# Softplus as one function of ScalarE in a four-layer kernel with a Mamba scan

## The chip, the core and the metric

The kernel runs on one core of a Trainium2 chip. The metric is the device time of one execution in microseconds (us), of which the median over several runs is taken. The core's engines work side by side, each through its own queue of instructions and in the order of that queue: PE multiplies matrices, DVE is the vector engine, ACT (ScalarE) evaluates functions, POOL is GpSimd, and SP only issues transfers. They wait for each other through semaphores.

## The reference

Eight images of 384 channels and 32 x 32 pixels pass through four layers. Layer 0 is a Mamba block that goes over the 1024 pixels forwards and backwards; layer 1 is a convolution block with linear attention and an MLP; layers 2 and 3 are 13 x 13 depthwise convolutions with a pointwise layer between them. The change lies in layer 0:

```python
dt, Bm, Cm = jnp.split(x_dbl, [dt_rank, dt_rank + D_STATE], axis=-1)
delta = jax.nn.softplus(jnp.einsum('blr,dr->bld', dt, dt_proj_w) + dt_proj_b)
A = -jnp.exp(A_log)
deltaA = jnp.exp(delta[..., None] * A)
deltaBu = (delta * u)[..., None] * Bm[:, :, None, :]
h = dA * h + dBu          # for each pixel, over 16 states of each channel
```

## The kernel before

All data is fp32. Channels lie on the 128 partitions in NC = 3 chunks (index c), and the 1024 pixels of an image in two halves of 512 (index h); index d is the direction, 0 forwards and 1 backwards.

**Stages.** `_layers01` computes layers 0 and 1 image by image. Three generators do the work of one image b. `front(b)` (line 572) normalizes, projects, convolves and ends with softplus; it writes u (u_d), z, B and C (bc_d), softplus (dl_d, called delta), delta times u (v_d) and a skip term (ud_d) to scratch in DRAM. `scan(b)` (line 695) reads them back, each channel replicated to four partitions for four of the 16 states at a time, and runs the recurrence. `layer1(b)` (line 877) does the output projection and layer 1. At the bottom of `_layers01`, front(0) comes first; then there is one round per image b, in which scan(b) gives the beat and pieces of front(b + 1) and layer1(b - 1) are recorded between its steps, in proportion to costs written by hand (90 and 325). Round 0 has no layer1, round 7 no front; layer1(7) follows the rounds, and then the two convolutions with the pointwise layer (lines 247 to 372).

**Order.** The order in which the lines are recorded is not yet the order in the queues: the framework's scheduler moves instructions at build time, so that for example the end of front(0) and the start of scan(0) are interleaved on every engine.[...] Which of ACT's instructions needs a load of another function table is also settled at build time, and such a load stands in ACT's queue as an instruction of its own.

**The scan.** For each of 12 units (d, h, c) and each of NR = 4 groups of states r, two pairs i of channel groups are treated. ACT computes da = exp(delta times A) (two instructions of 512 columns, line 776), DVE du = v times B (line 781, 1024 columns, into PSUM) and then two scans with `tensor_tensor_scan` (line 793), POOL multiplies the result hs by C (line 802), and PE sums over the states into acc (`sums`, line 736). There are 768 such pairs in all. A small copy (line 798) carries the state from the first half of the pixels to the second.

**Softplus** stands at the end of `front`. For each half h, line 652 projects onto dt, B and C, ACT copies that to xd (line 656), and then for each chunk c and direction d PE expands dt into a PSUM tile (line 667). ACT takes four passes over it: Abs with the bias into t (line 671), Relu with the bias into dl (line 672), exp(-t) (line 676) and ln(1 + t) (line 678), so that Relu plus Ln is softplus. The closure `deltas` is deferred by one `tick`: DVE adds the two (line 683), multiplies by u (line 684, result into t), POOL issues both transfers to DRAM (lines 685 and 686), DVE adds the u of both directions (line 687), and ACT scales that by D and sends it away (lines 689 and 690). Eight fronts with two halves, three chunks and two directions make 96 such tiles.

**Buffers.** `t2` is a ring of eleven SBUF tiles of 128 x 512 that `front` and `layer1` share (the MLP's hm also lives in it): the eleventh tile after takes the buffer again, and whichever instruction first writes it waits for the last reader, often a transfer. `psum` is a ring of two PSUM tiles named "mm", used by the dt matmuls, the projections, the small convolutions and the MLP's first product mf. The MLP of layer 1 alternates PE (mf, line 502), ACT's Gelu (hm, line 1062) and PE (mo, line 1064).

Of the kernel before, what the change touches and what calls it, by code (L numbers as in the profile page):

```python
# [9 lines left out]
AF = mybir.ActivationFunctionType  # L10
# [364 lines left out]
def _layers01(tc, nc, B, xv, x2_d, dram, ident, mean_w, eps5, eps6, one, half, minus1, vec, bns, bnt,  # L375
# [12 lines left out]
    with ExitStack() as ctx:  # L388
# [73 lines left out]
        def t2(name):  # L462
            return sp.tile([P, HALF], FP, tag="t2", name=name, bufs=N_T2)
# [4 lines left out]
        def a6(name):  # L468
            return sp.tile([P, NC, HALF], FP, tag="a6", name=name, bufs=N_A6)
# [80 lines left out]
        def rsqrt_mean(srcs, eps, name):  # L550

            stat = psum(f"{name}_s")
            for k, src in enumerate(srcs):
                for j in range(4):
                    nc.tensor.matmul(
                        stat[32 * j : 32 * j + 32, 0:P], mean_w[:, 0:32], src[:, j * P : (j + 1) * P],
                        start=(k == 0), stop=(k == NC - 1), skip_group_check=True,
                    )
            r = t2(f"{name}_r")[:, 0:P]
            nc.scalar.activation(r, stat[:, 0:P], AF.Ln, bias=eps)  # L560
            nc.scalar.activation(r, r, AF.Exp, scale=-0.5)
            ps = psum(f"{name}_b")
            for j in range(4):
                nc.tensor.matmul(
                    ps[:, j * P : (j + 1) * P], spread[:, j, :], r, start=True, stop=True,
                    skip_group_check=True,
                )
            return ps
# [3 lines left out]
        def front(b):  # L572

            xn = []
            for h in range(2):
                cols = bass.ts(h, HALF)
                xh = a6(f"xi_{b}_{h}")
                nc.sync.dma_start(xh, xv[b][:, :, cols])
                sqs = [t2(f"sq_{b}_{c}_{h}") for c in range(NC)]
                for c in range(NC):  # L580
                    nc.scalar.activation(sqs[c], xh[:, c, :], AF.Square)
                rstd = rsqrt_mean(sqs, eps6, f"ms_{b}_{h}")
                t, mid = image6(f"xn_{b}_{h}")
                for c in range(NC):
                    nc.vector.scalar_tensor_tensor(
                        mid[c], rows(xh[:, c, :]), vec("norm_w", c), rows(rstd), ALU.mult, ALU.mult
                    )
                put_image(xn_d, b % 2, h, t, nc.gpsimd)
                xn.append(mid)
                yield 3  # L590
            uo = u_d[b % 2].rearrange("(c p) i -> p c i", p=P)
            for e in range(2):
                w = wtile(inproj_t[:, e * C : (e + 1) * C], f"win_{b}_{e}")
                for h in range(2):
                    for m in range(NC):
                        ps = psum(f"in_{b}_{e}_{m}_{h}")
                        dense(ps, w, m, xn[h])
                        t = t2(f"uz_{b}_{e}_{h}_{m}")
                        if e == 0:
                            nc.scalar.copy(t, ps)  # L600
                            nc.scalar.dma_start(uo[:, m, 3 + h * HALF : 3 + (h + 1) * HALF], t)
                        else:
                            nc.scalar.activation(t, ps, AF.Silu)
                            nc.scalar.dma_start(zv[b][:, m, bass.ts(h, HALF)], t)
                        yield 3


            t3 = tapw(taps3, f"t3_{b}")
            for h in range(2):
                for c in range(NC):  # L610
                    xr = t2(f"xr_{b}_{h}_{c}")
                    nc.sync.dma_start(xr, xv[b][:, c, bass.ts(h, HALF)])
                    ps = conv3(xn_d, b % 2, h, c, t3, f"lc_{b}_{h}_{c}")
                    lc = t2(f"lg_{b}_{c}_{h}")
                    nc.scalar.activation(lc, ps, AF.Sigmoid, bias=vec("dw_b0", c))

                    def local(h=h, c=c, lc=lc, xr=xr):
                        nc.vector.tensor_mul(rows(lc), rows(lc), xn[h][c])
                        nc.vector.scalar_tensor_tensor(xr, lc, rs, xr, ALU.mult, ALU.add)
                        nc.gpsimd.dma_start(x1v[b][:, c, bass.ts(h, HALF)], xr)  # L620

                    defer(1, local)
                    yield 3


            for h in range(2):
                cols = bass.ts(h, HALF)
                ucs = [a6(f"uc_{b}_{h}_{d}") for d in range(2)]
                for c in range(NC):
                    uts = []  # L630
                    for j in range(4):
                        ut = sp.tile([P, 18 * (W + 2)], FP, tag="im", name=f"ut_{b}_{h}_{c}_{j}", bufs=N_IM)
                        src = bass.AP(
                            u_d.tensor, u_d[b % 2, 32 * (4 * c + j), h * HALF].offset,
                            [[UL, 32], [1, 4], [1, HALF + 3]],
                        )
                        nc.sync.dma_start(ut[:, 0 : HALF + 3], src)
                        uts.append(ut)
                    for d in range(2):
                        ps = psum(f"c1_{b}_{h}_{c}_{d}")  # L640
                        col32(
                            ps, lambda j, i: t1[:, d * NG + 4 * c + j, :],
                            lambda j, i: uts[j][:, 3 * d : 3 * d + HALF], 1,
                        )
                        nc.scalar.activation(ucs[d][:, c, :], ps, AF.Silu, bias=vec("conv1d_b", c))
                    yield 2

                xd = t2(f"xd_{b}_{h}")
                ps = psum(f"xd_{b}_{h}")
                for k in range(NC):  # L650
                    for d in range(2):
                        nc.tensor.matmul(
                            ps[64 * d : 64 * d + 64, :], wx[:, k, :], ucs[d][:, k, :],
                            start=(k == 0), stop=(k == NC - 1), skip_group_check=True,
                        )
                nc.scalar.copy(xd, ps)
                for d in range(2):
                    lo = 64 * d + DTR
                    nc.scalar.dma_start(bc_d[b, d][:, cols], xd[lo : lo + 2 * NST, :])
                yield 3  # L660

                for c in range(NC):
                    dls, ts = [], []
                    for d in range(2):
                        ps = psum(f"dt_{b}_{h}_{d}_{c}")
                        at = slice(64 * d, 64 * d + DTR)
                        nc.tensor.matmul(
                            ps, wdt[at, c * P : (c + 1) * P], xd[at, :], start=True, stop=True
                        )
                        t, dl = t2(f"sp_{b}_{h}_{d}_{c}"), t2(f"dl_{b}_{h}_{d}_{c}")  # L670
                        nc.scalar.activation(t, ps, AF.Abs, bias=vec("dt_b", c))
                        nc.scalar.activation(dl, ps, AF.Relu, bias=vec("dt_b", c))  # L672
                        ts.append(t)
                        dls.append(dl)
                    for t in ts:
                        nc.scalar.activation(t, t, AF.Exp, scale=-1.0)
                    for t in ts:
                        nc.scalar.activation(t, t, AF.Ln, bias=one)

                    def deltas(h=h, c=c, dls=dls, ts=ts, ucs=ucs):  # L680
                        for d in range(2):
                            dl, t = dls[d], ts[d]
                            nc.vector.tensor_add(dl, dl, t)
                            nc.vector.tensor_mul(t, dl, ucs[d][:, c, :])
                            nc.gpsimd.dma_start(dlv[b, d][:, c, bass.ts(h, HALF)], dl)
                            nc.gpsimd.dma_start(vv[b, d][:, c, bass.ts(h, HALF)], t)
                        nc.vector.tensor_add(ucs[0][:, c, :], ucs[0][:, c, :], ucs[1][:, c, :])
                        ud = t2(f"ud_{b}_{h}_{c}")
                        nc.scalar.activation(ud, ucs[0][:, c, :], AF.Copy, scale=vec("D", c))
                        nc.scalar.dma_start(udv[b][:, c, bass.ts(h, HALF)], ud)  # L690

                    defer(1, deltas)
                    yield 3

# [519 lines left out]
```

## Time and profile before

The median is 5797.18 us (5793.76 to 5818.33 over three runs); the profiled execution took 5805.1 us from first to last instruction, at a mean granted PE clock of 0.896.

| stretch (us from the start) | stage | PE busy | DVE busy | ACT busy |
|---|---|---|---|---|
| 150 to 212 | end of front(0) before the scan | 34.4 | 13.2 | 32.2 |
| 212 to 300 | front(0) and scan(0) interleaved | 53.5 | 46.0 | 62.5 |
| 300 to 550 | round 0 | 167.9 | 227.9 | 145.2 |
| 550 to 750 | round 0, softplus of front(1) | 108.7 | 179.4 | 119.3 |
| 4640 to 4785 | layer1(7) | 96.4 | 19.2 | 15.3 |
| 5075 to 5220 | first convolution | 145.0 | 27.1 | 8.6 |

Busy is the time in us in which an engine executed something in the stretch. In the slices of the profile each digit stands for one fortieth of the span, 145 us, in tenths. A group line gives line of code, engine, operation, output and inputs by name, shapes, count, then busy time and mean duration in ns, then the idle time of the engine directly before and what ended it. In the waits view a line reads: who waited (engine, output, line), for whom, us in total, times, longest.

### The profile page before, as it was taken

To read this page: it belongs to the slowest core of one execution; us is meant where nothing else is said; L and a number is where in the kernel's file an instruction comes from. 1 tells how busy PE (TensorE), PEld (TensorE's weight loads), DVE (VectorE), ACT (ScalarE), POOL (GpSimd) and SP (SyncE) were. 2 spreads that over 40 slices of the span, in tenths; PEclk is the share of its full clock that TensorE was granted. 3 is DMA by queue.
4 is the path that set the end of the run, shared out by engine and by line. 5 is a ranking of instruction groups with operands and counts; after the bars stand their busy time and mean duration, and the time that the engine had idled before them with its cause. 6 is when DMAs were issued, how large, how long until landed. Compare 5 with 4: busy or idle time off the path is not lost. (4 is left out here: it accounts for less than half of the span.)

```text
span 5805.1 us, 57844 instructions
## 1 busy us (share of the span) xinstructions
PE 4813.5 (83%) x19550; PEld 2091.8 (36%) x19550; DVE 3677.1 (63%) x3775; ACT 3064.5 (53%) x4116; POOL 2892.9 (50%) x1603
## 2 busy tenths in 40 slices
PE   4576579977988799879888997899779869899999
PEld 1121124322332243223322332233223324498498
DVE  0399997968687768776878786878678811011211
ACT  1656546874667557846784687468635613000211
POOL 3277676557554656565656564656466700110133
PEclk7687689988999899989999998899889989999999
DMA  9555476677567756764666467646643541366677
GB/s 299 185 176 178 145 247 194 230 188 216 187 197 202 216 173 193 168 204 134 191 205 189 141 175 186 190 140 176 179 145 120 135 96 45 95 165 158 196 166 150
DMA packets 528255, 1012.16 MB, mean 174 GB/s; under 512 B 60616, under 2 KB 196248, under 8 KB 527960
## 3 DMA queue, kind: packets, MB, share of 16 engines
q1 hardware_dynamic: 387952, 665.99, 38.5%
q0 software_dynamic: 71136, 248.53, 16.6%
q10 hardware_dynamic: 68872, 93.95, 5.1%
q8 instruction: 155, 2.54, 0.2%
q14 instruction: 140, 1.15, 0.1%
HBM read 763.86 MB, written 288.36 MB: 181 GB/s over the span
## 5 line engine op out<-in xcount | busy, mean ns | idle before, releaser
L802 POOL TENSOR_TENSOR hs<-hs,bct 128x1024 f32<-128x1024 f32 x768 | 2378.7, 3098 | 1180.4 <-DVE hs L793 665.8
L776 ACT ACTIVATE da<-dlt,neg_a 128x512 f32<-128x512 f32 x1536 | 1031.7, 714 | 848.8 <-DVE hs L793 756.8
L793 DVE TENSOR_TENSOR_SCAN hs<-da,carry,du 128x512 f32<-128x512 f32 x768 | 947.1, 1268 | 445.8 <-PE acc L736 211.0
L781 DVE TENSOR_TENSOR du<-vr,bct 128x1024 f32<-128x1024 f32 x768 | 1048.3, 1365 | 51.7 <-issue 21.7
L793 DVE TENSOR_TENSOR_SCAN hs<-da,du 128x512 f32<-128x512 f32 x768 | 901.2, 1208 | 153.9 <-ACT da L776 74.0
L736 PE MATMUL acc<-hs,selt 128*32 128x512 f32 x3072 | 736.5, 674 | 293.0 <-POOL hs L802 241.7
L1064 PE MATMUL mo<-hm,w 128*128 128x512 f32 x1152 | 562.5, 628 | 84.4 <-ACT hm L1062 60.8
L502 PE MATMUL mf<-ln,w 128*128 128x512 f32 x1152 | 545.7, 614 | 42.8 <-ACT dl L672 40.4
L736 PEld LDWEIGHTS acc<-hs,selt 128*32 128x32 f32 x3072 | 122.3, 115 | 722.2 <-POOL hs L802 391.6
L1064 PEld LDWEIGHTS mo<-hm,w 128*128 128x128 f32 x1152 | 214.9, 197 | 427.8 <-issue 255.1
L776 ACT ACT_TABLE_LOAD x265 | 340.0, 1283 | 39.2 <-DVE hs L793 26.7
L502 PEld LDWEIGHTS mf<-ln,w 128*128 128x128 f32 x1152 | 215.2, 194 | 358.9 <-issue 285.1
L316 PE MATMUL cv_b<-xt_b,toep 128*64 128x256 f32 x2688 | 304.5, 388 | 14.1 <-DVE xt_b L298 14.1
L316 PE MATMUL cv_a<-xt_a,toep 128*64 128x256 f32 x2688 | 304.6, 388 | 9.2 <-DVE xt_a L298 9.2
L502 PE MATMUL in<-xn,win 128*128 128x512 f32 x576 | 289.1, 633 | 26.0 <-ACT phi_k L874 24.2
L511 PE MATMUL dw<-dw_i,t3b 96*32 96x512 f32 x1152 | 238.0, 707 | 86.4 <-DMA dw_i<-h_d 86.3
L316 PEld LDWEIGHTS cv_b<-xt_b,toep 128*64 128x64 f32 x2688 | 282.5, 199 | 36.6 <-issue 16.2
L316 PEld LDWEIGHTS cv_a<-xt_a,toep 128*64 128x64 f32 x2688 | 282.4, 199 | 31.1 <-issue 10.4
L511 PE MATMUL lc<-lc_i,t 96*32 96x512 f32 x1152 | 218.1, 679 | 57.2 <-issue 28.8
L511 PE MATMUL c<-ut,t 128*32 128x512 f32 x768 | 195.2, 676 | 45.6 <-DMA ut<-u_d 32.1
L502 PE MATMUL op<-g,wo 128*128 128x512 f32 x288 | 143.1, 647 | 86.7 <-DMA g<-g_d 58.7
L1062 ACT ACTIVATE hm<-mf,biasf 128x512 f32<-128x512 f32 x192 | 130.7, 687 | 145.2 <-PE mf L502 143.5
(189 smaller groups left out, 5618.3 us busy)
## 6 DMA issues: line engine op xcount, KB each, us to landing
dlt<-dl_d SPq DMA_DIRECT2D x384, 256.0 KB, 4.5
vr<-v_d SPq DMA_DIRECT2D x384, 256.0 KB, 4.7
bct<-bc_d SPq DMA_DIRECT2D x256, 256.0 KB, 4.1
ut<-u_d SPq DMA_DIRECT2D x192, 257.5 KB, 5.0
lc_i<-xn_d SPq DMA_DIRECT2D x192, 228.8 KB, 4.9
dw_i<-h_d SPq DMA_DIRECT2D x192, 228.8 KB, 4.1
tp_d<-g_d POOLq DMA_DIRECT2D x64, 672.0 KB, 7.2
w<-w_d SPq DMA_DIRECT2D x64, 576.0 KB, 5.8
```

The source lines that it names most:

```text
L316: nc.tensor.matmul(ps[2 * H * e : 2 * H * (e + 1), 0:BW], tp[:, 2 * (g % (GB // 2)) + e, :, :, t].rearrange("p c j -> p (c j)"), rhs, star ...
L502: nc.tensor.matmul(ps, w[:, k, m * P : (m + 1) * P], rhs[k] if isinstance(rhs, list) else rhs[:, k, :], start=(k == 0), stop=(k == NC - 1),)
L511: nc.tensor.matmul(ps[32 * j : 32 * j + 32, :], lhs(j, i), rhs(j, i), start=(i == 0), stop=(i == taps - 1), skip_group_check=True,)
L736: nc.tensor.matmul(acc[32 * j : 32 * j + 32, :], selt, hs[j // 2][:, bass.ts(j % 2, HALF)], start=(r == 0), stop=(r == NR - 1), skip_group ...
L776: nc.scalar.activation(da[:, bass.ts(j, HALF)], dlt[:, bass.ts(j, HALF)], AF.Exp, scale=neg_a[:, g, r : r + 1],)
L781: nc.vector.tensor_mul(pairs(du), pairs(vt), bct[r][:, 0:1, :].to_broadcast([P, 2, HALF]),)
L793: nc.vector.tensor_tensor_scan(t[:, s][:, way], da[:, s][:, way], du[:, s][:, way], k_c if second else 0.0, ALU.mult, ALU.add,)
L802: nc.gpsimd.tensor_mul(pairs(t), pairs(t), bct[r][:, 1:2, :].to_broadcast([P, 2, HALF]))
L1062: nc.scalar.activation(hm, ps, AF.Gelu, bias=biasf[:, NC * i + f, :])
L1064: nc.tensor.matmul(acc[m], wb[:, f, m * P : (m + 1) * P], hm, start=(i == 0 and f == 0), stop=(i == FF // C - 1 and f == NC - 1),)
```

## The change

ScalarE has Softplus as a function of its own. One activation with the bias now writes dl from PSUM; Abs, Relu, Exp and Ln and DVE's addition are gone. Since t is no longer there when DVE multiplies by u, the closure draws a fresh tile v from the same ring. In the changed program Softplus stands in line 670, the multiplication in line 676, and later lines have numbers smaller by eight. Its purpose is to take passes off ACT and an addition off DVE.

```diff
                 for c in range(NC):
-                    dls, ts = [], []
+                    dls = []
                     for d in range(2):
...
-                        t, dl = t2(f"sp_{b}_{h}_{d}_{c}"), t2(f"dl_{b}_{h}_{d}_{c}")
-                        nc.scalar.activation(t, ps, AF.Abs, bias=vec("dt_b", c))
-                        nc.scalar.activation(dl, ps, AF.Relu, bias=vec("dt_b", c))
-                        ts.append(t)
+                        dl = t2(f"dl_{b}_{h}_{d}_{c}")
+                        nc.scalar.activation(dl, ps, AF.Softplus, bias=vec("dt_b", c))
                         dls.append(dl)
-                    for t in ts:
-                        nc.scalar.activation(t, t, AF.Exp, scale=-1.0)
-                    for t in ts:
-                        nc.scalar.activation(t, t, AF.Ln, bias=one)
-
-                    def deltas(h=h, c=c, dls=dls, ts=ts, ucs=ucs):
+
+                    def deltas(h=h, c=c, dls=dls, ucs=ucs):
                         for d in range(2):
-                            dl, t = dls[d], ts[d]
-                            nc.vector.tensor_add(dl, dl, t)
+                            dl, t = dls[d], t2(f"v_{b}_{h}_{d}_{c}")
                             nc.vector.tensor_mul(t, dl, ucs[d][:, c, :])
```

## The prediction, made before the changed kernel had run

> **What bounds the kernel now.** I first read the page: busy times and slices.
>
> ```profile
> PE 4813.5 (83%) x19550; PEld 2091.8 (36%) x19550; DVE 3677.1 (63%) x3775; ACT 3064.5 (53%) x4116; POOL 2892.9 (50%) x1603
> DVE  0399997968687768776878786878678811011211
> ACT  1656546874667557846784687468635613000211
> ```
>
> Over the span ACT (53%) looks harmless, but the slices show rounds of about four slices in the scan stage (about 212 to 4650 us), and once per round ACT rises to 7 or 8 tenths while DVE falls to 6 or 7. The chain of waits does not help: it reaches back only to 5017 us, through the two convolutions. So I went to the groups by line, for what the change touches:
>
> ```profile
> L678 ACT ACT_TABLE_LOAD x60 | 77.0, 1283 | 1.1
> L671 ACT ACTIVATE sp<-dt,pk 128x512 f32<-128x512 f32 x96 | 65.5, 682 | 106.9 <-PE dt L667 78.1 <-DMA dl_d<-dl 18.3 <-DMA ud_d<-ud 10.4
> L672 ACT ACTIVATE dl<-dt,pk 128x512 f32<-128x512 f32 x96 | 65.4, 681 | 0.1
> L678 ACT ACTIVATE sp<-sp,one 128x512 f32<-128x512 f32 x96 | 65.4, 716 | 0.7
> L676 ACT ACTIVATE sp<-sp 128x512 f32<-128x512 f32 x96 | 57.1, 628 | 0.4
> L676 ACT ACT_TABLE_LOAD x35 | 44.9, 1283 | 0.6
> L683 DVE TENSOR_TENSOR dl<-dl,sp 128x512 f32<-128x512 f32 x96 | 97.0, 1035 | 106.5 <-ACT sp L678 106.5
> ```
>
> Busy and mean duration stand after the first bar, idle time before the group after the second. These rows are all that softplus costs. The windows view then placed them: besides front(0), each of seven fronts has its twelve tiles within a stretch of 160 to 200 us. For the six rounds with both background jobs (1150:1310, 1760:1930, 2310:2480, 2880:3040, 3440:3600, 4020:4180), one row and the sum:
>
> ```profile
> core 0: us, PE busy (x) PEld busy (x) DVE busy (x) ACT busy (x) POOL busy (x), PEclk, DMA share, GB/s
> 2880.00:3040.00 160.00, 137.66 (x391) 44.77 (x390) 125.58 (x113) 139.72 (x174) 95.72 (x59) 0.94 0.64 198
> sum 980.00, PE 780.92 PEld 252.48 DVE 690.38 ACT 779.98 POOL 524.21; mean PE 130.15 PEld 42.08 DVE 115.06 ACT 130.00 POOL 87.37
> ```
>
> ACT is busy 780 of 980 us, as much as PE. Who waits there? From the whole kernel's waits view:
>
> ```profile
> DVE hs L793 <- ACT da L776: 254.0, 82, 16.4
> DVE dl L683 <- ACT sp L678: 106.5, 30, 24.1
> PE mo L1064 <- ACT hm L1062: 60.8, 40, 5.3
> ```
>
> In the six stretches alone, DVE's waits for ACT add up to 231.5 us (45.0, 51.3, 34.9, 27.9, 37.3, 35.1) and PE's to 104.0 us (24.5, 41.7, 8.8, 6.3, 12.4, 10.3). So in the softplus stretches ACT's queue is what the scan on DVE, and partly PE, stands behind; elsewhere it is not.
>
> **What the Trainium skill says.** "ScalarE: Activation LUTs", section "What ACT_TABLE_LOAD costs", prices a load at 1283 ns plus a DRAIN of about 1380 ns, and every function alike, about 93 ns more with a pointer bias. The trace agrees on 1283 ns and on durations (628 ns with immediates, 681 to 716 with a pointer bias), but not on the DRAIN: between the load at 189.24 us and the Exp at 190.54 there is only the load. The same page, section "Table sets: the hidden batching unit", says that Exp and Ln share one set and need one load. The trace differs: 35 loads stand before the Exp of softplus and 60 before the Ln. "Perfetto Trace Analysis", section "Tensor Engine Instruction (MATMUL, LD_WEIGHTS)", says that ACT and DVE are strict FIFO; the trace agrees where scans stop behind a softplus addition (below). No page prices Softplus.
>
> **The change part by part.** *ACT.* Removed: 65.5 + 65.4 + 57.1 + 65.4 = 253.4 us of activations, and 95 loads, 121.9 us. Added: 96 Softplus. The trace has none; from below the fastest op on this PSUM shape is the copy at L600, 577 ns, from above Ln, 716 ns. I take L671's 682 ns, same operands: 65.5 us. The loads I counted in the two built instruction orders: 61 before Softplus (78.3 us), and elsewhere 34 more before the scan's Exp, 3 more before Silu, 6 fewer before Gelu, 2 fewer each at L561 and L1015: 27 more, 34.6 us. In all 776 loads become 769. Net: -253.4 - 121.9 + 65.5 + 78.3 + 34.6 = -196.9 us, or 24.6 us for each of eight fronts.
>
> *DVE.* 96 additions go, 97.0 us: 8.4 in front(0), 16.7 in 550:750, 10.1 to 14.5 in each later stretch.
>
> *Buffers and waits.* Each channel chunk still draws five tiles from the ring of eleven t2, so its length costs nothing; but v's tile is now drawn when DVE multiplies, not when ACT begins. The waits for old transfers at L671 (18.3 + 10.4 us) can thus move to DVE, where the scans queue behind them, and behind those POOL's multiplications and PE's sums. Between zero and one transfer each (4.8 us to landing for v_d): I take zero, since the tile is asked for later than before, and most old ones land within 5 us. The two PSUM tiles "mm" come free after one operation and perhaps a load (0.68 to 1.97 us) instead of two (1.26 us spaced): no change taken. PE, POOL and the transfers keep their work, and their order shifts a little: at the round ends the scan stands up to one unit further ahead of the MLP.
>
> *Where it shows.* (a) front(0), where nothing hides it:
>
> ```profile
> 193.75 1.31 DVE L683 TENSOR_TENSOR dl<-dl,sp 128x512 f32<-128x512 f32 x2 [24.09 <-ACT sp L678]
> 205.70 1.23 DVE L781 TENSOR_TENSOR du<-vr,bct 128x1024 f32<-128x1024 f32 x1 [1.42 <-DMA vr<-v_d]
> 214.88 0.72 ACT L776 ACTIVATE da<-dlt,neg_a 128x512 f32<-128x512 f32 x1
> 215.64 1.22 DVE L793 TENSOR_TENSOR_SCAN hs<-da,du 128x512 f32<-128x512 f32 x1 [3.34 <-ACT da L776]
> ```
>
> ACT's first-half softplus runs from 186.80 to 209.77, and the first scan waits for an Exp behind it. With Softplus the first result is there at about 188.8 instead of 193.7, du about 5.6 us earlier (near 200), and ACT is free by then: first scan near 205, 10 us won. In the second half DVE has no scan from 246.2 to 266.4, its queue held by additions that wait for Ln; ACT takes 27 us there for 24 operations and five loads, and six operations with three loads each followed by one back to Exp should take some 12 us less of it. I take 12. Together 22 us.
> (b) The round of scan(0), stretch 550:750: DVE is busy 179.4 of 200 us, ACT 119.3. DVE bounds, so the additions count, 16.7 us; 15 taken.
> (c) Six rounds: ACT offers 24.6 us each. DVE's waits for ACT (231.5 / 6 = 38.6) would let all of it through; PE's (104.0 / 6 = 17.3) are what PE can win before it bounds itself. I take three quarters of 17.3, since some Gelu loads stay: 13 us each, 78 us.
> (d) The last scan, the last layer1 and the convolutions have no softplus: nothing.
> Sum: 22 + 15 + 78 = 115 us; 5797 - 115 = 5682.
>
> **Rivals.** *ACT all on the path*: 196.9 us come off, 5600 us. For it: 80% busy in the stretches. Against: a fifth idle, PE as busy. *PE and DVE bind, ACT is hidden there*: only (a) and (b), 37 us, 5760 us, or half of that (5778) if the ut loads hold up the start. For it: PE is busy 781 of 980 us. Against: the 104 us that PE waits for ACT. *The wait moves to DVE*: if each of the 96 v tiles waited 2 us, under half of one transfer's 4.8 us, 192 us would come on against 115 won: 5797 + 77 = 5874 us. The shifted order can work the same way, since 299 loads instead of 265 now stand right before an Exp whose da DVE needs. For it: DVE is in order and carries the scan. Against: only four such waits in 96 had any length before.
>
> **How the numbers follow.** Forecast (60 to 160 us won) 0.60; ACT all on the path 0.09; hidden 0.18, of which a bit over a third is under 29 us, 0.5%; moved wait or shifted order 0.13, of which 0.03 ends as no change. So faster 0.60 + 0.09 + 0.11 = 0.80, same 0.07 + 0.03 = 0.10, slower 0.10. The range: 5625 below (a bit over halfway from the forecast to the first rival), 5800 above, which takes in the hidden case and leaves out only the slower one.
>
> **What would show it.** Right: 96 Softplus near 682 ns with 61 loads; ACT some 197 us less busy, DVE 97; first scan near 205 us; scans at a higher rate in the softplus stretches and DVE's waits for da well under 254 us. Wrong: idle time of DVE before v's multiplication, put down to dl_d, v_d or mo; Softplus dearer than 0.72 us; rounds as long as before with PE's share up; or a lower PE clock.

## The result and the profile after

The changed kernel takes 5724.24 us (median of four runs, 5717.46 to 5741.58), where the kernel before took 5802.22 us beside it (the three runs given above and one more): a ratio of 0.987, interval 0.983 to 0.990. So 78 us came off (58 to 97 by the interval), 1.3%; 115 us (2.0%) had been forecast, with a range of 5625 to 5800 us. The two profiled executions are 65 us apart (5805.1 and 5739.7); what follows is read from them.

The changed kernel's page gives these busy times and slices:

```profile
PE 4793.9 (84%) x19550; PEld 2100.7 (37%) x19550; DVE 3602.0 (63%) x3679; ACT 2886.6 (50%) x3821; POOL 2872.7 (50%) x1603
DVE  0498887868887668676877785788578701111211
ACT  1555546764676368646774676467636612000211
```

ACT's share falls from 53 to 50%, but the pattern stays: once per round ACT still stands at 6 to 8 tenths and DVE falls to 5 or 6. The groups by line show what softplus costs now (busy time and mean ns after the first bar, idle time before the group after the second):

```profile
L768 ACT ACT_TABLE_LOAD x299 | 383.6, 1283 | 30.5 <-DVE hs L785 20.5 <-DVE biasf L848 3.2 <-DMA dlt<-dl_d 1.2
L676 DVE TENSOR_TENSOR v<-dl,uc 128x512 f32<-128x512 f32 x96 | 91.0, 980 | 29.6 <-ACT dl L670 20.6 <-DMA v_d<-v 6.1 <-DMA dl_d<-dl 2.6
L670 ACT ACT_TABLE_LOAD x61 | 78.3, 1283 | 25.5 <-DMA v_d<-v 14.0 <-DMA ud_d<-ud 9.4 <-ACT xd L656 0.9
L670 ACT ACTIVATE dl<-dt,pk 128x512 f32<-128x512 f32 x96 | 62.9, 685 | 32.5 <-PE dt L666 32.0
```

Softplus takes 685 ns, 3 ns more than the value taken for it, and its 61 loads and the 299 before the scan's Exp are those counted from the instruction order. DVE's idle time in front of v that is due to transfers is 8.7 us in all (6.1 + 2.6); another 23.4 us of such waits (14.0 + 9.4) stand on ACT, in front of the loads of Softplus.

The page's busy time of DVE fell by 75 us (3677.1 to 3602.0), not by the 97 of the additions, since the multiplication by u takes 91.0 us where it took 71.7 before. The trace shows why: 82 of the 96 multiplications take 680 ns on average, the other 14 between 1.5 and 2.9 us. Each of these 14 begins while POOL runs one of its products and ends 0.55 us after that product; none of the 82 begins with more than 0.03 us of a product left. One of the 14 is the first of the two multiplications in the second line here, which takes 2.83 us (a line gives start, duration, operation, idle time before):

```profile
243.14 3.24 POOL L794 TENSOR_TENSOR hs<-hs,bct 128x1024 f32<-128x1024 f32 x1 [1.73 <-DVE carry L790]
244.10 3.43 DVE L676 TENSOR_TENSOR v<-dl,uc 128x512 f32<-128x512 f32 x2
```

Before, 20 of the 96 additions took over 1 us, all of them under such a product, and only 4 of the multiplications behind them.

The windows view was taken of the softplus stretches, from the first small-convolution matmul (c, line 511) of the front to the end of the output projection (op) that follows it, in rounds 1 to 6. The sum row before was 1475 us with PE 1185.16, DVE 1034.65 and ACT 1112.43; after:

```profile
core 0: us, PE busy (x) PEld busy (x) DVE busy (x) ACT busy (x) POOL busy (x), PEclk, DMA share, GB/s
2794.00:3019.00 225.00, 195.15 (x638) 66.49 (x637) 162.82 (x161) 166.11 (x196) 136.56 (x78) 0.95 0.65 207
sum 1432.00, PE 1158.06 PEld 398.38 DVE 996.68 ACT 985.64 POOL 801.39; mean PE 193.01 PEld 66.40 DVE 166.11 ACT 164.27 POOL 133.57
```

ACT lost 127 us in these stretches, and they became 43 us shorter. Where the rest stayed is seen in the DVE waits over six whole rounds, from the end of the op of image 0 to that of image 6 (before 767 to 4214 us, after 737 to 4144 us). A line reads: who waited, for whom, us in total, times, longest. Before:

```profile
DVE hs L793 <- ACT da L776: 236.6, 79, 16.4
DVE hs L793 <- PE acc L736: 218.6, 48, 19.1
DVE dl L683 <- ACT sp L678: 60.3, 23, 11.0
DVE zr L749 <- PE acc L736: 34.1, 16, 4.4
DVE du L781 <- DMA vr<-v_d: 9.6, 2, 5.6
```

And after:

```profile
DVE hs L785 <- ACT da L768: 236.0, 72, 23.1
DVE hs L785 <- PE acc L728: 224.3, 44, 19.4
DVE du L773 <- DMA vr<-v_d: 55.8, 7, 19.1
DVE zr L741 <- PE acc L728: 45.4, 16, 7.5
DVE du L773 <- DMA bct<-bc_d: 25.9, 3, 9.7
```

The wait for Ln (60.3 us, the softplus addition in line 683) is gone with the addition that did the waiting. The large wait, scans for their da, is what it was: 236.6 and 236.0 us. And 72 us of waits for transfers (81.7 against 9.6) are new. DVE, which carries the scan, is busy 2590.70 instead of 2651.20 us in these rounds, and the rest of them, in which it is idle, grew from 796 to 816 us.

### The profile page after: what moved, and what is told of

It is laid out like the page before. It is cut to its first block, busy times and chain, and to the rows that moved or that the text cites. A ratio compares the mean times of both kernels' runs of the same rounds, so it can differ in the third digit from the quotient of the medians.

```text
span 5739.7 us, 57345 instructions
## 1 busy us (share of the span) xinstructions
PE 4793.9 (84%) x19550; PEld 2100.7 (37%) x19550; DVE 3602.0 (63%) x3679; ACT 2886.6 (50%) x3821; POOL 2872.7 (50%) x1603
## 5 line engine op out<-in xcount | busy, mean ns | idle before, releaser
L502 PE MATMUL in<-xn,win 128*128 128x512 f32 x576 | 302.2, 658 | 39.5 <-ACT phi_k L866 35.0
L511 PE MATMUL c<-ut,t 128*32 128x512 f32 x768 | 175.2, 655 | 40.4 <-DMA ut<-u_d 37.7
```

The lines of the kernel that those rows point to most:

```text
L502: nc.tensor.matmul(ps, w[:, k, m * P : (m + 1) * P], rhs[k] if isinstance(rhs, list) else rhs[:, k, :], start=(k == 0), stop=(k == NC - 1),)
L511: nc.tensor.matmul(ps[32 * j : 32 * j + 32, :], lhs(j, i), rhs(j, i), start=(i == 0), stop=(i == taps - 1), skip_group_check=True,)
```

## The experiments

Each kernel was timed beside the kernel before; "won" is the median of before less its own. The kernel before took 5787.84 us beside e1 to e4, 5789.64 beside e5 to e8, 5804.43 beside e9 to e11 and 5784.36 beside e12, so that traces of different groups can differ by some 20 us without a cause in the kernel. The changed kernel's own difference, 78 us, has an interval of 58 to 97; a few us more or less than that say nothing. For the missing 37 us theory 1 was that ACT, in its strict order, now stands behind DVE: the scaling ud waits 120.6 us for DVE's uc in the changed kernel, 20.1 before. Its rivals were that of ACT's microseconds only a part, some 0.4 of each, reaches the end; and that ACT does not count at all, PE and the order of the instructions deciding alone.

**Softplus without its own table** (e1). Exp stands in Softplus' place; nothing else changes.

```diff
-                        nc.scalar.activation(dl, ps, AF.Softplus, bias=vec("dt_b", c))
+                        nc.scalar.activation(dl, ps, AF.Exp, bias=vec("dt_b", c))
```

> The changed kernel with Exp, the scan's own function, in place of Softplus (delta becomes exp(x) and not ln(1 + exp(x)), so that the function is left incomplete). The pass stays; 92 table loads go (769 to 677 in the built order), 118 us less on ACT. Theory 1, ACT's freed time has turned into a wait of ACT for DVE's sum of u ahead of the skip term (120.6 us in the changed kernel, 20.1 before): little changes, about 5710 us. Rival 2, ACT's busy time is still what bounds, at the rate seen so far (78 us won for 197 us less ACT work, 0.4): 47 us more off, about 5677 us. Rival 3, PE and the round's order bind now: about 5720 us.

Measured: 5666.89 us, ratio 0.978 (0.977 to 0.980), 121 us won. ACT's busy time is 2763.7, 123 us less than in the changed kernel, for another 43 us: 0.35 us per us. DVE's waits in the six rounds (733 to 4084 us):

```profile
DVE hs L785 <- PE acc L728: 333.9, 62, 22.1
DVE xx L882 <- PE op L502: 124.7, 6, 25.7
DVE hs L785 <- ACT da L768: 67.9, 28, 7.1
```

Here the wait for da at last falls, by 168 us, but the rounds get only 56 us shorter (3407 to 3351): two waits for PE grow by 176 us (224.3 to 333.9 and 58.2 to 124.7), while those for transfers halve (82 to 41).

**The scaling ud on DVE, its transfer on POOL** (e2).

```diff
-                        nc.scalar.activation(ud, ucs[0][:, c, :], AF.Copy, scale=vec("D", c))
-                        nc.scalar.dma_start(udv[b][:, c, bass.ts(h, HALF)], ud)
+                        nc.vector.tensor_scalar_mul(ud, ucs[0][:, c, :], vec("D", c))
+                        nc.gpsimd.dma_start(udv[b][:, c, bass.ts(h, HALF)], ud)
```

> The changed kernel with the skip term ud scaled on DVE and its transfer issued by POOL, so that ACT never waits for DVE's sum of u. ACT loses 34.5 us of passes and the wait of 120.6 us, gains 27 loads (35 us); DVE gains 48 passes, some 20 to 35 us. Theory 1 (that wait is where the gain went): 40 us or more off the changed kernel, below 5690 us. Rival 2 (ACT's busy time counts): no gain, since ACT's work is the same in sum, 5725 to 5735 us. Rival 3 (PE and the order bind): 5725 to 5745 us.

Measured: 5708.12 us, 0.985 (0.983 to 0.987), 80 us won, as the changed kernel. ACT's wait for uc is away (there is no such operation on it), and no gain shows: theory 1, which asked for 40 us or more, is not borne out. It is not ruled out in full, since the build placed 27 more loads, so that ACT's busy time stayed at 2890.9 us, and DVE is busy 57 us more (3602.0 to 3658.5).

**The old four passes without DVE's addition** (e3): dl is Relu alone, v is made from it.

```diff
-                            nc.vector.tensor_add(dl, dl, t)
```

> The kernel before with its four passes, only DVE's addition left out (delta is then the Relu part alone, v the Ln part times u). What DVE's 97 us are worth by themselves. By the prediction's sum, which credited DVE with 15 us in round 0 and little elsewhere: about 5780 us. If DVE carries most of the gain: about 5740 us. If it carries nothing: 5800 us.

Measured: 5769.86 us, 0.996 (0.995 to 0.998), 18 us won. When round 0 ends 14 us are there: the op of image 0 ends at 753 us instead of 767. In the trace the six rounds are another 29 us shorter (3418 to 3447), more than the medians bear out.

**Each Softplus twice** (e4).

```diff
                         nc.scalar.activation(dl, ps, AF.Softplus, bias=vec("dt_b", c))
+                        nc.scalar.activation(dl, ps, AF.Softplus, bias=vec("dt_b", c))
```

> The changed kernel with each Softplus pass made twice: 96 more passes and 33 more loads, 108 us more on ACT, all of it in the softplus stretches. Rival 2 (ACT's busy time counts, 0.4 per us): about 43 us slower than the changed kernel, 5767 us. Theory 1 (ACT has waits of its own there that take it up): 10 to 20 us slower, about 5740 us. Rival 3: about 5730 us.

Measured: 5874.7 us, 1.014 (1.012 to 1.016), 87 us lost, 165 us over the changed kernel. ACT's busy time rose by 102 us (2886.6 to 2988.9), so each microsecond put on costs 1.6, if all of the loss is put down to ACT; the granted PE clock was lower too (0.891 in the profiled execution, 0.903 in the changed kernel's), and its part was not separated. DVE's wait for da rises to 311.5 us in the six rounds and PE's for POOL's products, which the scans feed, from 35.1 to 132.2 us. ACT is not hidden: adding to its queue costs more than its time, taking away gives less.

**Softplus in fronts 0 and 1 only** (e5). The six later fronts keep the old passes.

```diff
+                    if b <= 1:
...
+                            nc.scalar.activation(dl, ps, AF.Softplus, bias=vec("dt_b", c))
...
+                    else:
...
+                            nc.scalar.activation(t, ps, AF.Abs, bias=vec("dt_b", c))
```

> Softplus only in front(0) and front(1), the four passes and the addition in the six later fronts: this splits the forecast's steps (a) and (b) from step (c). Time before is some 5790 us, the changed kernel stood 78 us under it. If (a) and (b) are worth what the round anchors of the two traces show at the end of round 0 (30 us), this kernel comes to 5760 us. If the start's 24 to 30 us are lost again by the last front, since they only shift when the rest meets, it stays near 5785. If most of the whole gain is made there, it comes to 5725. Round 0 should end at about 737 us as in the changed kernel.

Measured: 5765.19 us, 0.996 (0.994 to 0.998), 24 us won. Round 0 ends at 738 us, 29 us early. So the forecast's steps (a) and (b) are worth 24 us by the medians and 30 by the end of round 0, of 37, and the rest of the shortfall is step (c).

**Softplus, with an addition on DVE** (e6): delta is added to itself, so it is doubled.

```diff
                             dl, t = dls[d], t2(f"v_{b}_{h}_{d}_{c}")
+                            nc.vector.tensor_add(dl, dl, dl)
                             nc.vector.tensor_mul(t, dl, ucs[d][:, c, :])
```

> The changed kernel, with an addition on DVE kept where the old one stood (delta is added to itself, so delta is doubled): ACT's part of the change alone. Leaving the addition out of the old kernel alone brought 18 us. If the two parts add up, this kernel stands 18 us above the changed one, 60 us under the kernel before: 5728 us where before is 5788. If DVE has become the tighter bound once ACT is relieved, its 97 us of additions count in full and it comes to about 5790 or more. If DVE's time is hidden beside ACT's, it is equal to the changed kernel, 5710.

Measured: 5716.39 us, 0.988 (0.986 to 0.989), 73 us won. The kept additions put 125 us on DVE's busy time (3602.0 to 3727.5) and cost 5 us of 78, which is within the interval. Round 0 ends at 750 instead of 737 us, so 13 us are lost where DVE bounds; the six rounds are then 28 us shorter than in the changed kernel (3379 to 3407), with DVE's wait for da at 175.1 instead of 236.0 us and its waits for transfers at 31. In the rounds the additions cost nothing that shows; the order of the instructions differs as well.

**Two thirds of the MLP's first product left out, old and changed** (e7, e8). Only k = 0 is multiplied; 768 matmuls go, all of them in layer1.

```diff
-                        dense(ps, wa, f, xns[h])
+                        x0 = xns[h][0] if isinstance(xns[h], list) else xns[h][:, 0, :]
+                        nc.tensor.matmul(ps, wa[:, 0, f * P : (f + 1) * P], x0, start=True, stop=True)
```

> The kernel before, with two of the three matmuls of the MLP's first product left out (only k = 0 is multiplied; 768 matmuls, some 370 us of PE in all, 46 us per layer1). It is the base line of the next run. If PE sets the length of the rounds by itself, some 300 us come off (5490); if the scan on DVE and ACT sets them, under 150 (5640 or more).

> The changed kernel with the same two thirds of that product left out. The difference to the run before it is what Softplus is worth when PE has 46 us less to do in each round (counting its loads, ACT is relieved of 212 us here, against 197 us in the original pair). If PE was the second bound that cut six rounds' gain from 13 to 7 us, the difference grows from 78 to 120 us or more. If PE was not it, and ACT's microseconds simply count 0.4 each, the difference is 80 to 90 us. If the gain was cut by DVE's own queue and its waits for transfers, it stays at 78 us or falls.

Measured: the old kernel with the cut 5726.97 us, 0.989 (0.987 to 0.991), 63 us won; the changed one 5599.77 us, 0.967 (0.966 to 0.969), 190 us won. With the cut, Softplus is worth 127 us instead of 78. The six rounds tell it more sharply:

| six rounds, us | all of the product | a third of it |
|---|---|---|
| four passes | 3447 | 3443 |
| Softplus | 3407 | 3330 |

PE's cut, 174 us of its busy time in these rounds (2936.37 to 2762.53), brings 4 us beside the four passes; 180 us (2919.00 to 2738.57) bring 77 us beside Softplus. Beside the four passes DVE's waits for PE fall too (371 to 337 us), but those for transfers grow as much (10 to 46). What else moves there: the cut kernels have 97 and 109 fewer loads on ACT (679 and 660), so that ACT is busy 117 and 132 us less in the six rounds; the granted PE clock is lower (0.878 and 0.888 in the profiled executions, against 0.896 and 0.903); and the order shifts. The pair is no test of PE alone. DVE's waits in the changed kernel with the cut (736 to 4066 us):

```profile
DVE hs L785 <- ACT da L768: 255.2, 52, 14.6
DVE hs L785 <- PE acc L728: 185.7, 29, 21.3
DVE zr L741 <- PE acc L728: 48.7, 14, 7.5
DVE du L773 <- DMA vr<-v_d: 32.9, 10, 9.2
DVE xx L882 <- PE op L502: 16.7, 5, 13.0
```

Against the changed kernel the waits for PE fall (224.3 to 185.7 and 58.2 to 16.7), those for transfers too (82 to 33.5); the wait for da does not, although ACT has 132 us less to do.

**Six Softplus side by side, dt taken out of PSUM by DVE or by ACT** (e9, e10). This is the same function with 17 or 18 instead of 61 loads before Softplus. Below is the first; in the second, `nc.scalar.activation(dl, ps, AF.Identity, bias=vec("dt_b", c))` stands in the second line.

```diff
-                        nc.scalar.activation(dl, ps, AF.Softplus, bias=vec("dt_b", c))
+                        nc.vector.tensor_scalar(dl, ps, vec("dt_b", c), None, ALU.add)
                         dls.append(dl)
+                    every.append(dls)
+                gate = wp.tile([P, 1], FP, tag="gate", name=f"gate_{b}_{h}", bufs=2)
+                nc.vector.tensor_scalar(gate, every[-1][-1][:, 0:1], 0.0, None, ALU.mult)
+                for dls in every:
+                    for dl in dls:
+                        nc.scalar.activation(dl, dl, AF.Softplus, bias=gate)
+                for c, dls in enumerate(every):
```

> The same function with fewer table switches: DVE takes dt out of PSUM and adds the bias, for all six tiles of a half, and the six Softplus, which read SBUF, get their bias (zero) from a column that DVE computes from the last of the six, so that all become ready together and the build puts them side by side. Loads before Softplus fall from 61 to 17, all loads from 769 to 694: 96 us less on ACT, some 100 us more on DVE. By the rate of 0.4 us per us of ACT that leaving away Softplus' own table showed, and with DVE's additions as cheap as the run with the kept addition showed them (4 us): 35 us under the changed kernel, 5675 where before is 5789. If the time of DVE counts here as it did in the kernel before (18 us), 5690. If the burst of six on ACT and six on DVE holds up the scan, no gain or a loss: 5710 or more.

> The same grouping, but ACT itself takes dt out of PSUM (Identity with the bias, 96 passes of some 0.6 to 0.7 us, 58 to 66 us). Loads fall to 691 (100 us less), so ACT is relieved of only 34 to 42 us and DVE gets nothing. By the rate of 0.4: 15 us under the changed kernel, 5697. If it is the loads as such that hold up the scan (long stops between two Exp), not the sum of ACT's time, it gains as much as the run with DVE's passes, 5675. If the burst of six holds up the scan, 5710 or more.

Measured: 5750.15 us, 0.991 (0.989 to 0.992), and 5763.23 us, 0.992 (0.991 to 0.994): 54 and 41 us won, both less than the changed kernel, although ACT is busy 100 and 48 us less than there. The first kernel's groups, then its waits in the six rounds (751 to 4153 us):

```profile
L667 PE MATMUL dt<-xd,wdt 24*128 24x512 f32 x192 | 95.9, 800 | 31.3 <-DVE dl L671 29.6 <-ACT xd L656 1.6
L678 ACT ACT_TABLE_LOAD x17 | 21.8, 1283 | 0.3
```

```profile
DVE hs L793 <- PE acc L736: 237.2, 45, 18.8
DVE hs L793 <- ACT da L776: 145.1, 45, 10.6
DVE xx L890 <- PE op L502: 72.7, 10, 21.9
PE dt L667 <- DVE dl L671: 28.0, 17, 6.8
```

The wait for da falls by 91 us, and the rounds stay as long as the changed kernel's (3402 us to 3407; round 0 ends 14 us later): DVE is busy 79 us more (2669.25 to 2590.70), waits 25 us more for PE, and PE, in its order, now stands before dt until DVE has emptied the PSUM tile (28.0 us). With ACT's own passes (e10) the wait for da falls as far (144 us), and the waits for PE grow by 56 us.

**v drawn early** (e11), right behind dl.

```diff
-                        dls.append(dl)
+                        dls.append((dl, t2(f"v_{b}_{h}_{d}_{c}")))
...
-                            dl, t = dls[d], t2(f"v_{b}_{h}_{d}_{c}")
+                            dl, t = dls[d]
```

> The changed kernel, but the tile v is drawn from the ring right behind dl, where the old kernel drew its t, instead of when DVE multiplies; same instructions, same loads (769). If the wait for an old transfer that the forecast took as zero (DVE's 8.7 us before v, 6 us of it in the start) costs the 37 us that are missing, this kernel gets some of them back, 5690 or less. If the wait costs what it measures, it comes within 8 us of the changed kernel, 5704 to 5716.

Measured: 5722.51 us, 0.986 (0.984 to 0.987), 82 us won, as the changed kernel within its interval. DVE's waits for transfers before v are 8.3 us (7.1 + 1.2) instead of 8.7, so this order hardly moved the wait: the point at which the tile is drawn is not where the missing microseconds are. What the wait itself costs is not shown.

**The skip term added by DVE instead of PE** (e12), built on e11; the function is the same.

```diff
-                if r == 0:
+                if r == 0 and d == 1:
                     nc.tensor.matmul(acc, ident, y0, start=False, stop=False, skip_group_check=True)
...
-                    yt = s2(f"yt_{b}_{h}_{c}")
-                    nc.scalar.copy(yt, acc)
-                    nc.scalar.dma_start(yfv[b][:, c, cols], yt)
+                    nc.vector.tensor_add(y0, acc, y0)
+                    nc.scalar.dma_start(yfv[b][:, c, cols], y0)
```

> The kernel with v drawn early, and in the forward direction the skip term y0 no longer goes into the sum by a matmul with the identity: DVE adds it when it takes the finished sum out of PSUM (into y0's own tile), in place of ACT's copy. The function is the same. PE loses 96 of 192 such matmuls (750 ns each as the changed kernel's trace shows: 64 us less, and some 16 us of weight loads), ACT 48 copies (28 us less) against seven more loads (9 us), DVE gets 48 additions (679 ns for the like on the backward direction: 33 us more). If PE is the second bound, its microseconds count as in the pair with the cut product (some 250 us less of PE and 110 us won beside Softplus: 0.45): with ACT's at 0.4 that is 36 us under the kernel with v drawn early, 5685 where before is 5800. If PE is not it: 8 us, 5712. If the new wait of DVE for the finished sum (56 us in all on the backward direction, for the same number of sums) or the longer life of y0 in its ring of three holds up the scan, 5730 or more.

Measured: 5739.14 us, 0.992 (0.991 to 0.994), 45 us won, worse than without. PE is busy 50 us less in the six rounds than in e11 (2878.46 to 2928.57), and these last 3389 instead of 3393 us; round 0 ends 8 us later. PE's waits (748 to 4137 us):

```profile
PE acc L728 <- POOL hs L793: 92.0, 28, 15.5
PE acc L728 <- DVE y L737: 31.7, 11, 5.2
```

The first was 33.5 us in e11, the second is new. So 50 us less on PE brought 4 here. Whether the new waits took the rest back was not tried by itself.

## Why the prediction was right and wrong

**Right: size of the edit on ACT, and the sign.** By the groups the forecast's -196.9 us on ACT is -199.5: the 253.4 us of four passes less the 62.9 of Softplus, and nine microseconds of loads. (The page's busy time, which counts overlapping passes once, fell by 178; two activations in a row show 1.26 us where two single ones have 0.69 each.) On DVE 75 us went instead of 97, as shown above. "ScalarE: Activation LUTs" of the Trainium skill, section "What ACT_TABLE_LOAD costs", says that every function costs alike; the 685 ns of Softplus beside 682 for Abs agree. Its DRAIN of about 1380 ns is again not seen: the first Softplus starts at 189.55, when a load of 1.28 us has begun at 188.25, and a load at 196.16 begins right at the end of a Softplus (195.46 and 0.69 us).

**Step (a), the start: 16 instead of 22 us, by another way.** Round 0 ends 30 us early, and 13 to 14 us of that are the additions (e6: 750 against 737; e3: 753 against 767), which leaves 16 for ACT's part. That this is near the forecast is luck, since the first scan did not move to 205 us. The timeline of the changed kernel (start, duration, operation, idle time before it):

```profile
189.55 1.26 ACT L670 ACTIVATE dl<-dt,pk 128x512 f32<-128x512 f32 x2
194.12 1.07 POOL L678 DMA_DIRECT2D v_d<-v  x2
203.38 0.51 SPq L720 DMA_DIRECT2D vr<-v_d  x1
203.46 0.69 DVE L676 TENSOR_TENSOR v<-dl,uc 128x512 f32<-128x512 f32 x1 [6.07 <-DMA v_d<-v]
203.99 10.18 SPq L637 DMA_DIRECT2D ut<-u_d  x6
206.82 0.72 ACT L768 ACTIVATE da<-dlt,neg_a 128x512 f32<-128x512 f32 x1
214.22 0.59 SPq L720 DMA_DIRECT2D vr<-v_d  x1
217.55 1.23 DVE L773 TENSOR_TENSOR du<-vr,bct 128x1024 f32<-128x1024 f32 x1 [12.80 <-DMA vr<-v_d]
218.88 2.33 DVE L785 TENSOR_TENSOR_SCAN hs<-da,du 128x512 f32<-128x512 f32 x2
```

The first da now begins at 206.82, 8 us ahead of the one that the first scan waited for before (214.88), but du waits for v's transfers, and the first scan comes at 218.88, 3 us later than before. This path stood in the forecast as if transfers kept their time, and they did not: v's first transfer to DRAM, which POOL issues behind four transfers of dl, takes 9.2 us from issue (194.12) to landing, where it took 3.1 before (from 196.22), and the second half of vr is issued only at 214.22, because in SP's queue six loads of u stand before it, of which one waits 6.3 us for PE. Before, the two halves of vr were issued side by side at 199.32. The wait for the ring's old tile, taken as zero, is 6.07 us on DVE here, at the sixth tile, which the first scan does not need. What was won came behind it: in the first half by scans that no longer wait for da, then in the second half, where no scan ran until 266.38 before (the gap began at 239.7 already, when the scans from 237.35 ended, and not at 246.2) and six now do from 249.86 on. By 300 us the changed kernel has begun 29 scans, the old one 18.

**Step (b), the additions in round 0: right.** 15 us were forecast, 13 to 14 measured (front(0)'s additions included).

**Step (c), six rounds of 13 us: the term that was mis-sized.** It measured 40 us instead of 78 (3447 to 3407 in the traces, 6.7 a round), and by the medians 54 (78 less the 24 of e5). The forecast took as room what PE waits for ACT, 17.3 us a round, and let three quarters of it go. In the softplus stretches of the windows view above these waits are 138 us before (47.6, 48.5, 9.6, 8.7, 13.2, 10.3) and 136 after (44.0, 36.1, 15.7, 12.6, 16.2, 11.4), so none of it went. In part another ACT instruction took the place of softplus, as for the MLP's first product mf over the six rounds, before and after:

```profile
PE mf L502 <- ACT dl L672: 40.4, 12, 15.2
PE mf L502 <- ACT uc L645: 1.2, 1, 1.2
```

```profile
PE mf L502 <- ACT dl L670: 28.9, 6, 7.0
PE mf L502 <- ACT uc L645: 22.0, 7, 5.0
```

The 40 us are DVE's account of the six rounds: 60 us less busy and 20 us more idle. In the idle time, the waits for ACT fell by 55 us (307 to 252; the one for Ln, 60.3, is gone, the one for da unchanged) and those that no other engine ends by 22 (39 to 17), while those for transfers rose by 72 (10 to 82) and those for PE by 23 (371 to 394). Two assumptions of the step fail there. DVE's waits for ACT "would let all of it through", but the larger part of them, the waits for da, did not shrink though ACT had 127 us less to do in the stretches. And of DVE's relief (60, 55 and 22 us) 95 us, two thirds, came back, mostly as waits for vr and bct, which stand in no part of the sum. The wait that the third rival feared, on DVE in front of v, stayed at 8.7 us in all; most waits for old tiles remained on ACT (28.7 us before L671, 23.4 now).

**What bounds in its place.** By the table of e7 and e8, taking off PE's work in layer1 wins nothing in these rounds beside four passes and 77 us beside Softplus, where DVE's waits for PE fall by 87 us (394 to 307). That speaks for PE cutting Softplus' gain short, as the rival "PE and DVE bind" has it, but does not show it, since ACT's loads, the clock and the order moved along, and e12, with 50 us less on PE, has rounds only 4 us shorter than e11. It is not PE alone either, as e1 wins another 43 us with PE's work unchanged. Neither ACT nor PE is the bound by itself; DVE's scan waits for the one, and when that wait is taken away (e1: 168 us less for da) it waits for the other (176 us more for PE). The exchange rates differ from run to run: ACT gave 0.44 us per us of the page's busy time in the change (78 of 178), 0.35 in e1, 0.66 with PE's load cut (127 of 193), and took 1.6 in e4.

**Left open.** Why the wait for da stays at 236 us in the changed kernel and falls in e1, e2, e6, e9 and e10 is not settled: these kernels differ in the order of instructions as well. e11, with the same instructions and loads, has rounds 14 us shorter than the changed kernel, and e5, whose six later fronts are the old ones, 13 us shorter than the kernel before, so differences of that size say nothing about a cause. That the new waits for vr and bct come from scans that run ahead of their transfers was not tried by itself in the rounds. No version of the same function beats the changed kernel by more than the interval.

## What to carry to other kernels

When several engines feed one in-order engine, add up that engine's busy time and waits over whole rounds, before and after: a wait that has gone is a gain only as far as no other has grown, and here transfers and PE took back more than the wait for Ln had cost. What an engine waits for another in the profile is not the room that relieving the other opens: the wait on which a whole forecast term rested went from 138 to 136 us. And grouping table loads, or shifting passes to the engine with idle time, must be weighed against whom the moved pass holds up: 75 loads fewer (e9) ended 24 to 28 us slower than leaving them.

## What the runs showed of the hardware that was not expected

Softplus does not share a loaded table with its neighbours here: 61 loads for 48 pairs of tiles, and 34 more before the scan's Exp, so each pair carries about two loads (2.6 us) for 1.37 us of work; with Exp in its place 17 loads stood before it. The multiplication v by u, 128x512, took 980 ns on average in the changed kernel (91.0 us), and 1101 and 1231 ns in e9 and e4, where the same multiplication behind the addition took 768 (71.7 us) before; a single one at the start takes 0.69 us. The long ones go with POOL: of those over 1 us, all 14 in the changed kernel, 16 of 19 in e9 and all 24 in e4 began under one of POOL's running products, and all but one of these ended 0.55 us after it. So a DVE instruction that is long in the profile need not have more work; no run took POOL's products away to test it.
